# Turning the normalized rows of an adaLN transformer block on VectorE and the DMA queues instead of TensorE

## The chip, the core and the metric

One core of a Trainium2 chip runs the whole program. The time is the device time of one execution in microseconds (us); of the kernel before there are three timed runs, 3591.07, 3591.7 and 3596.67 us, median 3591.7. The engines are named as the profile names them: PE (TensorE matmul), PEld (its weight loads), DVE (VectorE), ACT (ScalarE), POOL (GpSimd) and SP (SyncE, which here issues the DMAs). L201 is line 201 of the kernel before. Where the text speaks of the changed kernel's lines it says so.

## What is computed

The input x has 8 sequences of 1024 tokens of width 512, all float32. Each token passes one transformer block whose two layer norms are modulated by a condition vector:

```python
mod = silu(condition) @ Wada + bada
sh_a, sc_a, gt_a, sh_m, sc_m, gt_m = split(mod, 6, axis=1)
xm = layernorm(x, g1, be1) * (1 + sc_a) + sh_a
x = x + gt_a * attention(xm, Wqkv, Wproj, bproj)      # 16 heads of 32, causal
xm = layernorm(x, g2, be2) * (1 + sc_m) + sh_m
x = x + gt_m * (gelu(xm @ W1 + b1) @ W2 + b2)         # 512 -> 2048 -> 512
```

A layer norm needs a token's 512 numbers in one row (a partition), so that mean and variance run along the row. The matmuls that follow need the numbers transposed: a channel per partition and the tokens along the row. This document is about how the rows are turned.

## The kernel before, in words

**Blocks and sets.** The work is cut into NB = 16 blocks of 512 tokens, two to a sequence. Block n has two sets of normalized rows: a{n} ahead of its attention and m{n} ahead of its MLP, 32 sets in all. A set is 4 tiles of 128 tokens by 512 channels.

**One set.** `normalize` (L547) reads the tiles: mean and variance on DVE (`bn_stats`, `bn_aggr`, L555 and L556), the square root on ACT (L563), reciprocal and offset on DVE (L565, L566), and the normalization as four activations on ACT (L580). ACT holds one table of functions at a time; root, exp and gelu lie in different tables, so a root costs a table load there and the next exp or gelu another. Root and apply are "excursions": jobs that are held back and run one at a time beside an attention unit. `modulated` (L615) then turns the set: for each of 4 chunks of 128 channels, 4 transposes by PE against the identity (L641) into one of the three linear PSUM banks, and one evacuation with gain and shift on DVE (L645) or ACT (L651) into the tile xm. Differences of parts of xm (T1 to T4) follow, which the 7-product (Strassen) form of the matmuls reads.

**Matmuls.** Almost all linear work goes through `matmul` (L194 to L201): four instructions that each fill 32 columns of the array. A product of the 7-product form is 4 such calls, 16 instructions. Float32 matmuls appear twice in the trace, once per pass; the transposes appear once.

**Two streams on PE.** A planner inside the kernel writes out the order of everything by hand. It keeps a modelled clock per engine (`now`), the time at which each datum is written (`written`) and each buffer left (`left`), and prices such as MM = 853 ns for two `matmul` calls and TR = 108 ns for a transpose. The attention stream (`attend`, scores, exp, weights times v, row sums) is written out in its own order; between its units the linear stream (`linear`, the steps of `plan[w]`) is fed in. `step_aside` does linear work as long as attention would wait, or until the linear stream has caught up with its `due`, which grows by each unit's need times a `rate`. The rate is `planned_time(n)`, the summed `costs` of the block's linear steps, over the block's attention need. Steps wait for guards: v of an even block waits until attention has left the block before ("free for v"), the output projection until its block is attended, mt (set m) until v is done.

**Attention's own limits.** Scores and exponents share one PSUM tile (`st`), so each unit waits until DVE has reduced the scores (L1406) or ACT has taken the exponent (L1493). There are three slots for exponents; POOL masks the diagonal ones (L1498) and adds the exponents of a group up (L1594, four additions a unit), and a slot is free only after that. `finish` (L1531) sums over keys by matmuls with ones (L1539), takes the reciprocal on DVE in four parts (L1554) and multiplies. If the linear stream is far away and no bank is in use, `scores_by_heads` (L1357) does a scores unit in the linear banks.

**Weights.** A ring of 9 tiles of 256 KB holds the linear weights. `fetch` (L319) issues a load as soon as the slot's last matmul has been written out; all loads, the x rows and the results are issued by SP in that one order.

Of the kernel before, what the change touches and what calls it, by code (L numbers as in the profile page):

```python
# [9 lines left out]
F32 = mybir.dt.float32  # L10
# [12 lines left out]
def kernel(  # L23
# [173 lines left out]
    def matmul(ps, lhsT, rhs, start, stop, reads=(), bank=None):  # L197

        for j in range(HPG):
            r = slice(j * hd, (j + 1) * hd)  # L200
            nc.tensor.matmul(  # L201
                ps[r, :], lhsT[:, r], rhs, start=start, stop=stop, skip_group_check=True
            )
        n = 1
        for d in rhs.shape[1:]:
            n *= d
        note_pe(2 * COLUMN * n, "columns", reads, [] if bank is None else [("l", bank)])
# [19 lines left out]
    def mlp_steps(n):  # L227
# [7 lines left out]
        + [("mod", 3), ("at", 2), ("v", 1), ("mod", 4), ("columns_m",), ("k", 2), ("gates", "m")],  # L235
    }
    late = []
    for w in range(1, NB):
# [7 lines left out]
        if w == NB - 1:  # L246
            steps = late[:1] + [("load_xr", n)] + rows_a + [("proj", n), ("mt", n)] + late[1:]
            steps += [("v", w)] + rows_m + own + m[3:6]
            late = m[6:]
        else:  # L250

            steps = late + [("v", w), ("load_xr", n)] + rows_a + [("proj", n), ("k", w + 1)]
            if w == 1:
                steps = [("load_xr", n)] + rows_a + [("proj", n)]
            steps += [("mt", n), ("q", w + 1)] + rows_m + own
            at = [("at", w + 2)] if w + 2 < NB else []
            if blocks[w][1] == 0:

                steps += m[3:5]
                late = m[5:6] + at + m[6:]  # L260
            else:
                steps += m[3:6] + at
                late = m[6:]
# [108 lines left out]
    def load_x(n, pool, tag):  # L372
        b, h = blocks[n]
        tiles = []
        for t in range(NTT):
            xt = pool.tile([P, D], F32, tag=tag, name=f"{tag}_{n}_{t}", bufs=NTT)
            nc.sync.dma_start(xt, x[b, h * TB + t * P : h * TB + (t + 1) * P, :])
            tiles.append(xt)
        return tiles

    x_pre = {0: load_x(0, tmp, "hat")}
# [11 lines left out]
    nc.gpsimd.memset(ones, 1.0)  # L393
    minus_ones = const.tile([P, P], BF16, tag="minus_ones", name="minus_ones")
# [23 lines left out]
    def modulation(i):  # L418
        at = take(4)
        part = {kf: halves(j) for kf, j in zip(RAW, at)}  # L420
# [39 lines left out]
    def gates(kind):  # L460

        i, bias = GATES[kind]
        at = take(4)
        part = {kf: halves(j) for kf, j in zip(RAW, at)}
# [44 lines left out]

    pool_jobs = []  # L510
# [23 lines left out]
    def hurry():  # L534

        while jobs and due(jobs[0][1]) <= now["PE"] + 500:
            jobs.pop(0)[0]()
        while excursions and due(excursions[0][1]) <= now["PE"] + 500:
            excursions.pop(0)[0]()
# [4 lines left out]
    def normalize(tiles, key, sources):  # L544
# [6 lines left out]
        got = []  # L551

        def statistics(t):
            st = small.tile([P, nc.vector.BN_STATS_DIM], F32, tag="st", name=f"st_{key}_{t}")
            nc.vector.bn_stats(st, tiles[t])  # L555
            nc.vector.bn_aggr(mv[:, t, :], st)  # L556
            note("DVE", 850, [sources[t]], [("mv", key)])
            if t == NTT - 1:
                excursion(root, [("mv", key)])
                excursion(apply, [("rstd", key)])  # L560
# [8 lines left out]
        def apply():  # L569
            for t, xt in enumerate(tiles):  # L570
                xh = xt
                if key[0] == "m":
                    xh = tmp.tile([P, D], F32, tag="hat", name=f"xh_{key}_{t}", bufs=NTT)
                if key == "a0" and t % 2:
                    nc.vector.tensor_scalar(
                        xh, xt, rstd[:, t : t + 1], offset[:, t : t + 1], ALU.mult, ALU.add
                    )
                    note("DVE", 700, [("rstd", key)], [("hat", key, t)])
                else:
                    nc.scalar.activation(  # L580
                        xh, xt, AF.Identity, bias=offset[:, t : t + 1], scale=rstd[:, t : t + 1]
                    )
                    note_act(800, None, [("rstd", key)], [("hat", key, t)])
                got.append(xh)
            hats[key] = got
# [4 lines left out]
    def normalize_tile(xt, key, t, source):  # L590
# [12 lines left out]
        def apply():  # L603
# [3 lines left out]
            xh = tmp.tile([P, D], F32, tag="hat", name=f"xh_{key}_{t}", bufs=NTT)  # L607
            nc.scalar.activation(xh, xt, AF.Identity, bias=offset, scale=rstd)
            note_act(800, None, [("rstd", key, t)], [("hat", key, t)])
            hats.setdefault(key, []).append(xh)  # L610

        return apply

    def modulated(key, gain, shift, b, guards):
        for t in ("B11", "B21", "B22", "T1", "T2", "T3", "T4"):  # L615
            written[key, t] = NEVER
        yield [("hat", key, 0), *guards], [BANK]
# [15 lines left out]
        at = {t: (key, t) for t in part}  # L633
        for c in range(NC):
            if c:
                yield [("hat", key, 0)], [BANK]
            bank = lin_bank()
            for t in range(NTT):
                if t:
                    yield [("hat", key, t)], []  # L640
                nc.tensor.transpose(banks[bank][:, ts(t, P)], got[t][:, ts(c, P)], ident)  # L641
                note_pe(TR, "whole", [("hat", key, t)], [("l", bank)])
            writes = [at["B11"], at["T1"]] if c < 2 else [at["B21"], at["B22"]]
            if sooner([("l", bank)], writes, 770, 780) == "DVE":
                nc.vector.tensor_scalar(  # L645
                    xm[:, c, :], banks[bank], gain[:, c, b : b + 1], shift[:, c, b : b + 1],
                    ALU.mult, ALU.add,
                )
                note("DVE", 770, [("l", bank)], writes)
            else:  # L650
                nc.scalar.activation(  # L651
                    xm[:, c, :], banks[bank], AF.Identity,
                    bias=shift[:, c, b : b + 1], scale=gain[:, c, b : b + 1],
                )
                note_act(780, None, [("l", bank)], writes)
            live[bank] = False
# [48 lines left out]
    def preparation():  # L705
# [15 lines left out]
        while loaded:  # L721
            if todo:
                load(*todo.pop(0))
            w, i, got, ready = loaded.pop(0)
            for out, a, b, op, name in IN_PLACE:
# [161 lines left out]
    def project_out(n):  # L887
# [48 lines left out]
        if not last:  # L936
            normalize(tiles, f"m{n}", [("xr", n, t) for t in range(NTT)])

    def up(step):
# [16 lines left out]
        if (n, q) == (0, 0):  # L956
            yield ["prepared"], []
# [30 lines left out]
    def down(n, part):  # L988
# [19 lines left out]
        def product(operand):  # L1008
# [3 lines left out]
            for i in range(NQ):  # L1012
                p = next(at)
                for k in range(2):
                    c = 2 * i + k
                    hT = hTs[n, 2 * kh + c // NC][:, c % NC, tokens]
                    for m in range(2):
# [3 lines left out]
                        else:  # L1021
                            yield [], []
                        matmul(
                            banks[bank][:, ts(m, HB)], hT[:, ts(m, P)], halves(p)[:, k, :],
# [45 lines left out]
        if part == 0:  # L1070
            yield [("g", n, 0), ("g", n, 1)], []
# [50 lines left out]
    def perform(step):  # L1122
# [9 lines left out]
        elif kind == "load_xa":  # L1132
            x_pre[step[1]] = load_x(step[1], tmp, "hat")
# [36 lines left out]
        elif kind == "preps":  # L1170
            prepared[0] = [preparation(), 0.0]
            written["prepared"] = NEVER
# [46 lines left out]
    def work():  # L1219

        if linear_wait() == NEVER:
            run_jobs(True)
            run_excursions()
# [6 lines left out]
        run_jobs()  # L1230
        run_pool_jobs()
# [18 lines left out]
    def step_aside(reads, writes):  # L1250
# [14 lines left out]
        run_jobs()  # L1265
        run_pool_jobs()
# [188 lines left out]
    free_p = list(range(3))  # L1455
    outs, totals = {}, {}
# [74 lines left out]
    def finish(n, g):  # L1531
# [3 lines left out]
        step_aside([("acc", n, g)], [BANK])  # L1535
        bank = lin_bank()
        for j in range(HPG):
            r = slice(j * hd, (j + 1) * hd)
            nc.tensor.matmul(banks[bank][r, :], ones[:, :hd], acc[:, j, :], start=True, stop=True)  # L1539
        note_pe(2 * COLUMN * TB, "columns", [("acc", n, g), ("p", slot)], [("l", bank)])  # L1540
        free_p.append(slot)
# [22 lines left out]

        def quotient():
# [16 lines left out]
    def add_weights(n, g, parts, pT, slot):  # L1582

        acc, first = totals[n, g]
# [67 lines left out]
    def close(n, g, parts, pT, slot, last):  # L1652
# [6 lines left out]
        elif parts[0][0] > 0:  # L1659
            free_p.append(slot)  # L1660
        if parts[0][0] == 0:
            totals[n, g] = (pT, slot)
            if (n, g) in shared:
# [3 lines left out]
                free_p.append(slot)  # L1667
# [100 lines left out]
```

## Time and profile before

| | us |
|---|---|
| profiled execution, whole | 3596.93 |
| its span, first to last instruction | 3594.9 |
| median of the three timed runs | 3591.7 |
| PE busy | 3520.8 |
| DVE busy | 2077.3 |
| POOL busy | 2045.1 |
| PEld busy | 1768.4 |
| ACT busy | 1326.4 |

The span is one execution by the hardware profiler. Busy time is the union of an engine's instructions; PE's are pipelined, so that the step from one start to the next, not the duration, tells what an instruction costs PE. The chain of waits follows the work that ended last backwards through whatever released each step. The profile's tables name groups of instructions by line, engine and tile; "idle before" is what the engine waited ahead of them and for whom. The mean granted clock of the execution was 0.993.

### The profile page before, as it was taken

The numbers are of one execution on the slowest core, as the hardware profiler recorded it, in microseconds if no ns is written. First come the engines' busy times: TensorE is split into PE (matmuls) and PEld (weight loads), VectorE is DVE, ScalarE is ACT, GpSimd is POOL, SyncE is SP. The second block draws the span as 40 slices with busy tenths as digits, with TensorE's granted clock in tenths as the row PEclk, the third lists the DMA queues.
The fourth block names the chain that finished last, engine by engine and source line by source line (L and its number), as shares of the span: only waits on it lengthen the run. The fifth ranks groups of instructions, "written<-read, shape, count | busy, mean of one in ns | idle before, by whom it ended". The sixth has DMA issues, their size and how long they took to land.

```text
span 3594.9 us, 120999 instructions
## 1 busy us (share of the span) xinstructions
PE 3520.8 (98%) x54821; PEld 1768.4 (49%) x54821; DVE 2077.3 (58%) x2316; ACT 1326.4 (37%) x1388; POOL 2045.1 (57%) x2187
## 2 busy tenths in 40 slices
PE   8989999999999999999999999999999999999999
PEld 4434445445554455544555445454554545445445
DVE  5766575464755647465464655746557455564663
ACT  2335334253433523335243351424524244232421
POOL 2666745665456754667536665456654566544660
PEclk9989999999999999999999999999999999999999
DMA  6643333434334343433434334343343433335334
GB/s 198 204 133 106 115 98 108 129 100 130 112 113 119 104 131 113 128 98 100 135 108 148 92 95 132 107 142 103 97 128 105 142 101 101 125 93 156 90 112 137
DMA packets 307893, 430.33 MB, mean 120 GB/s; under 512 B 25900, under 2 KB 176236, under 8 KB 307380
## 3 DMA queue, kind: packets, MB, share of 16 engines
q1 hardware_dynamic: 307264, 422.56, 38.6%
q8 instruction: 431, 7.06, 0.8%
q14 instruction: 82, 0.67, 0.1%
q10 hardware_dynamic: 116, 0.03, 0.0%
HBM read 394.12 MB, written 28.38 MB: 118 GB/s over the span
## 4 chain that ended last, share of the span: by engine, by line
PE 88%; DVE 4%; POOL 3%; ACT 3%; issue 1%; DMA 0%; SPq 0%; DVEq 0%; ACTq 0%; POOLq 0%
PE bank L201 61%; PE sc L1389 8%; PE po L1521 7%; PE st L1481 6%; PE st L1469 2%; POOL pT L1594 2%; DVE mx L1406 2%; PE bank L1539 1%; PE bank L641 1%; ACT pT L1493 1%; POOL xr L161 1%; DVE hT L1003 0%; ACT hT L945 0%; DVE xr L158 0%; PE bank L1444 0%
## 5 line engine op out<-in xcount | busy, mean ns | idle before, releaser
L1594 POOL TENSOR_TENSOR pT<-pT,pT 128x384 f32<-128x384 f32 (+2 forms) x1266 | 1196.8, 981 | 393.1 <-PE po L1521 207.2
L1493 ACT ACTIVATE pT<-st 128x2048 f32<-128x2048 f32 x288 | 541.0, 1878 | 849.3 <-PE st L1481 738.7
L201 PE MATMUL bank<-w,hT 128*32 128x256 f32 x14336 | 806.7, 381 | 1.0 <-ACT rec L1545 0.9
L1406 DVE TENSOR_REDUCE mx<-sc 128x4 f32<-128x2048 f32 (+3 forms) x380 | 658.7, 1754 | 144.9 <-PE sc L1389 137.7
L201 PEld LDWEIGHTS bank<-w,hT 128*32 128x32 f32 x14336 | 455.5, 110 | 339.1 <-issue 41.6
L201 PE MATMUL bank<-xm_m,w 128*32 128x256 f32 x8192 | 497.6, 380 | 3.2 <-ACT xm_m L651 3.0
L201 PE MATMUL bank<-t_m,w 128*32 128x256 f32 x6144 | 392.2, 381 | 0.1
L1498 POOL TENSOR_SCALAR_AFFINE_SELECT pT<-pT 128x512 f32<-128x512 f32 x256 | 167.3, 671 | 393.1 <-ACT pT L1493 393.1
L201 PEld LDWEIGHTS bank<-xm_m,w 128*32 128x32 f32 x8192 | 254.4, 110 | 231.9 <-issue 63.5
L1389 PE MATMUL sc<-kT,qT 32*128 32x512 f32 (+3 forms) x3040 | 330.2, 522 | 7.6 <-DVE mx L1406 7.0
L1403 DVE TENSOR_TENSOR sc<-sc,mask 128x1024 f32<-128x1024 f32 (+1 forms) x159 | 161.6, 1016 | 277.2 <-PE sc L1389 243.6
L1521 PE MATMUL po<-pT,v 128*32 128x512 f32 (+3 forms) x3072 | 306.7, 494 | 12.6 <-POOL pT L1498 12.6
L1481 PE MATMUL st<-qT,kT 32*128 32x512 f32 (+3 forms) x3072 | 302.8, 489 | 0.0
L201 PEld LDWEIGHTS bank<-t_m,w 128*32 128x32 f32 x6144 | 187.0, 110 | 197.4 <-issue 78.6
L201 PE MATMUL bank<-xm_a,w 128*32 128x256 f32 x3968 | 242.0, 382 | 0.0
L201 PE MATMUL bank<-w,qT 128*32 128x512 f32 x2048 | 239.4, 598 | 0.0
L1554 DVE RECIPROCAL rec<-rec 128x128 f32<-128x128 f32 x256 | 226.1, 920 | 5.7 <-ACT rec L1545 5.7
L1389 PEld LDWEIGHTS sc<-kT,qT 32*128 32x128 f32 x3040 | 130.4, 184 | 176.0 <-ACT pT L1493 83.2
L201 PE MATMUL bank<-t_a,w 128*32 128x256 f32 x2944 | 189.4, 381 | 0.0
L1493 ACT ACT_TABLE_LOAD x88 | 112.9, 1283 | 203.1 <-PE st L1481 202.6
L193 DVE TENSOR_TENSOR hT<-bank,u_u 128x512 f32<-128x512 f32 x192 | 128.6, 684 | 94.4 <-PE bank L201 93.5
L1425 POOL CAST mcols<-mx 128x16 bf16<-128x16 f32 x63 | 16.5, 262 | 290.7 <-DVE mx L1420 160.5
(207 smaller groups left out, 3640.8 us busy)
## 6 DMA issues: line engine op xcount, KB each, us to landing
w<-in_L_cond_W_dram SPq DMA_DIRECT2D x384, 256.0 KB
w<-kept_up_S SPq DMA_DIRECT2D x256, 256.0 KB
w<-kept_down_S SPq DMA_DIRECT2D x256, 256.0 KB
w<-kept_qkv_S SPq DMA_DIRECT2D x180, 256.0 KB
w<-in_L_cond_Wqkv_dram SPq DMA_DIRECT2D x147, 256.0 KB
hat<-in_x_dram SPq DMA_DIRECT2D x64, 256.0 KB
w<-in_L_cond_Wproj_dram SPq DMA_DIRECT2D x64, 256.0 KB
xr<-in_x_dram SPq DMA_DIRECT2D x64, 256.0 KB
```

The lines of the kernel that those rows point to most:

```text
L193: nc.vector.tensor_tensor(out, src, other, op)
L201: nc.tensor.matmul(ps[r, :], lhsT[:, r], rhs, start=start, stop=stop, skip_group_check=True)
L1389: nc.tensor.matmul(sc[:, j, c0 : c0 + w], qTs[n][r, gg, ts(qt, P)], keys_of(n, kh)[r, gg, :w], start=True, stop=True, skip_group_check=True,)
L1403: nc.vector.tensor_tensor(place, place, shape_of.to_broadcast(place.shape), ALU.add)
L1406: nc.vector.tensor_reduce(maxima[n, gg][:, kh, qt, :], sc[:, :, c0 : c0 + w], axis=AX.X, op=ALU.max)
L1469: nc.tensor.matmul(st[:, j, c0 : c0 + w], minus_ones[r, :], row[r, TB - w :], start=(c0 == 0), stop=False, skip_group_check=True,)
L1481: nc.tensor.matmul(st[:, j, c0 : c0 + w], kT[r, gg, ts(k % NTT, P)], qT[r, gg, TB - w :], start=False, stop=True, skip_group_check=True,)
L1493: nc.scalar.activation(pT[:, :, :used], st[:, :, :used], AF.Exp, scale=scale)
L1498: nc.gpsimd.affine_select(diagonal, diagonal, pattern=[[0, HPG], [1, P]], compare_op=ALU.is_ge, fill=0.0, base=0, channel_multiplier=-1,)
L1521: nc.tensor.matmul(po[r, TB - w :], v[:, k % NTT, g * P + j * hd : g * P + (j + 1) * hd], pT[:, j, c0 : c0 + w], start=(k == 0), stop=last ...
L1554: nc.vector.reciprocal(some, some)
L1594: nc.gpsimd.tensor_tensor(into, into, pT[:, j, c0 : c0 + w], ALU.add)
```

## The change

Sets a0, a1, m0, m14 and m15 are still turned by PE. The other 27 (a2 to a15, m1 to m13) are turned thus: each of the 4 row tiles is transposed on DVE in squares of 32 by 32 into the tile xm, which serves as staging; 16 DMAs of 32 partitions by 2 KB, issued by SP, gather the squares from xm back into the set's row tile, where channels then lie along the partitions; and the evacuation with gain and shift reads that tile in SBUF, not PSUM. So that the squares fall right, x rows of the turned a sets are loaded with 32 partitions per tile of 128 tokens, and the tokens of the turned m sets stay permuted, which `down` undoes by the order in which it takes its stationary columns. The four row tiles become one tile, hat, with one buffer.

After the opening, the root is no activation: POOL computes (variance + eps) to the power -0.5 and the offset in four small instructions. The four applications become jobs of their own that go to DVE or ACT, whichever the planner thinks sooner.

In block 0's last head group the three later exponent tiles are not added on POOL; PE sums them with the first by more matmuls with ones, and the quotient is taken on DVE.

Some steps move. k of block 2 goes from the plan of block 0 to that of block 1, ahead of proj 0; mt goes ahead of k in later blocks; u of block 0 waits only for the up weights ("prepared up").

```diff
-            steps = late + [("v", w), ("load_xr", n)] + rows_a + [("proj", n), ("k", w + 1)]
+            steps = late + [("v", w), ("load_xr", n)] + rows_a + [("proj", n), ("mt", n), ("k", w + 1)]
             if w == 1:
-                steps = [("load_xr", n)] + rows_a + [("proj", n)]
-            steps += [("mt", n), ("q", w + 1)] + rows_m + own
+                steps = [("load_xr", n)] + rows_a + [("k", w + 1), ("proj", n), ("mt", n)]
+            steps += [("q", w + 1)] + rows_m + own
...
+    by_pe = ("a0", "a1", "m0", f"m{NB - 2}", f"m{NB - 1}")
+    def hat_tile(key):
+        return tmp.tile([P, NTT, D], F32, tag="hat", name=f"hat_{key}", bufs=1)
...
+        def power():
+            nc.gpsimd.tensor_scalar(rstd, mv[:, :, 1], EPS, None, ALU.add)
+            nc.gpsimd.tensor_tensor(rstd, rstd, minus_half, ALU.pow)
+            nc.gpsimd.tensor_scalar(offset, mv[:, :, 0], -1.0, None, ALU.mult)
+            nc.gpsimd.tensor_tensor(offset, offset, rstd, ALU.mult)
+            note("POOL", 1500, [("mv", key)], [("rstd", key)])
...
+    def turn(key, rows, xm):
+        small_blocks = xm.rearrange("p c n -> p (c n)")
+        by_tile = small_blocks.rearrange("p (m h t i) -> p h m t i", m=NTT, h=NC, t=NTT)
+        def turn_tile(t):
+            into = by_tile[:, :, :, t, :]
+            nc.vector.transpose(into, rows[:, t, :].rearrange("p (h m i) -> p h m i", m=NTT, i=Q))
+            note("DVE", 620, [("hat", key, t)], done)
+        for t in range(NTT):
+            add_job(lambda t=t: turn_tile(t), [("hat", key, t)], key[0] == "m")
+        yield [("blocks", key)], []
+        for m in range(NTT):
+            for a in range(NTT):
+                nc.sync.dma_start(rows[ts(m, Q), a, :], small_blocks[ts(a, Q), ts(m, D)])
+        written["turned", key] = now["PE"] + GATHERING
+        yield [("turned", key)], []
+    GATHERING = 9000
...
         for c in range(NC):
+            if turned:
+                source, out = ("turned", key), xm[:, c, :].rearrange("p (a x) -> p a x", x=P)
+                values = got[:, :, ts(c, P)]
+            else:
...
...
+        terms = [(0, TB, acc, slot)] + [(c0, w, pT, slot) for parts, pT, slot in more for _, c0, w, _ in parts]
+        for i, (c0, w, term, held) in enumerate(terms):
+            for j in range(HPG):
+                nc.tensor.matmul(
+                    banks[bank][r, TB - w :], ones[:, :hd], term[:, j, c0 : c0 + w],
```

The line `costs = {"at": 16 * TR, "mt": 16 * TR, ...}`, from which the linear stream's rate comes, is not changed.

## Prediction

> **What bounds the kernel.** The page first: the busy line and PE's slices.
>
> ```profile
> PE 3520.8 (98%) x54821; PEld 1768.4 (49%) x54821; DVE 2077.3 (58%) x2316; ACT 1326.4 (37%) x1388; POOL 2045.1 (57%) x2187
> ...
> PE   8989999999999999999999999999999999999999
> ...
> PEclk9989999999999999999999999999999999999999
> ...
> PE 88%; DVE 4%; POOL 3%; ACT 3%; issue 1%; DMA 0%; SPq 0%; DVEq 0%; ACTq 0%; POOLq 0%
> ```
>
> PE is busy 98% and carries 88% of the chain that ended last; DVE has 1518 us to spare and ACT 2269. Work taken off PE shortens the run unless something new makes PE wait, and PE's 74 us of idle time are the most that any other edit could win. So I read second what a transpose costs PE, in the timeline of PE: set a4, turned without a break, and the two halves of set m1.
>
> ```profile
> 844.53 2.18 PE L641 MATMUL bank<-ident,hat 128*128 128x128 f32 x16
> 846.73 0.85 PE L201 MATMUL bank<-w,hT 128*32 128x256 f32 x11
> ...
> 504.98 1.09 PE L641 MATMUL bank<-ident,xh_m 128*128 128x128 f32 x8
> 506.50 0.64 PE L201 MATMUL bank<-xm_m,w 128*32 128x256 f32 x8 [0.43 <-ACT xm_m L651]
> ```
>
> The step from the first transpose to the next matmul is the price: 846.73 - 844.53 = 2.2 us a set. The second half of m1 took 1.52 for 8, of which 0.43 is waiting for the evacuation. Third, the windows view of the slow stretch near the start (columns: window, length, busy and count of PE, PEld, DVE, ACT, POOL, granted clock, DMA share, GB/s).
>
> ```profile
> 177.00:207.00 30.00, 20.00 (x108) 8.05 (x106) 28.29 (x36) 2.46 (x2) 15.64 (x15) 0.60 0.82 285
> 400.00:430.00 30.00, 29.33 (x492) 15.77 (x488) 19.76 (x18) 5.58 (x5) 26.97 (x28) 0.97 0.36 105
> ```
>
> Between 177 and 207 PE is idle a third of the time and runs at a granted clock of 0.60; DVE is full: the linear stream is waiting for block 0 to be attended, and scores alone go on at DVE's pace. At 400 to 430 POOL is nearly full (27.0 of 30) and PE is kept busy by linear work.
>
> **The change, term by term** (us of span; plus is slower).
>
> 1. *Transposes off PE.* 27 sets of 16 leave. The 12 sets a4 to a15 cost 2.2 each (26). a2 and a3, cut up by waits for evacuations, cost 3.4 and 4.6 in their timelines (8). The m sets alternate between two halves of 1.02 and 1.52 (2.54; m1 and six more) and 12 + 4 at 1.73 and 0.59 (2.32; six): 18 + 14 = 32. Sum 66; some of the waiting in it will return as waiting elsewhere, so **-63**, bounds -47 (432 bare transposes at 0.109, the usual step) and -70 (with 0.11 for the switch into each run, the step before it being 0.31 and not 0.20).
>
> 2. *The hole at 177 to 207.* At full clock and without gaps its instructions would take about 10 of the 30 us. The changed order puts 28 calls of k(2) and the projection between the scores, 2.6 to 4.5 us of PE work after each unit against DVE's 3.0 to 3.6 (2.29 to reduce, 0.66 to 1.21 for the mask). The exponent sums on PE spare POOL 12 additions and cost PE three more terms, 4 x (0.17 + 0.11 + 0.06) = 1.4. Together **-15**, bounds -20 and 0 (the hole stays).
>
> 3. *The hole moves.* k(2) was what kept the end of block 1 supplied. In the changed order of PE's instructions, the last five exponent units around the end of block 1 and three scores units have no linear instruction between them, 14.5 us of PE work by the steps above. There each unit is paced by POOL: four additions of 512 columns at
>
> ```profile
> L1594 POOL TENSOR_TENSOR pT<-pT,pT 128x512 f32<-128x512 f32 x504 | 648.6, 1320 | 223.8 <-ACT pT L1493 183.3 <-PE po L1521 38.0
> ```
>
> 1.32 make 5.3 a unit. From the group's second unit to its sum POOL has 3 x 5.3 + 6 (diagonal) + 7 (the cut ones) = 29; PE's work there is 15 to 19: **+14**, bounds +6 and +24 (with a lowered clock after it).
>
> 4. *Smaller holes.* `costs` still charges the linear stream 16 TR for each at and mt, so the rate is 3.5 us a block too high and linear work runs ahead until a guard stops it. The order shows three such stretches more (two of three or four units ahead of the first products of m3 and m7, one of five at block 15's start): each unit takes its PE work, 1.15, and 1.88 for the exponent (L1493), or 0.96 and 2.3 for the reduction, with nothing beside it: **+8**, bounds +3 and +16.
>
> 5. *The end.* Now 80 linear instructions (8.9 us) lie between the last sum with ones and the last projection, and 88 more between that sum and the last unit ahead of it. In the changed order all of them come earlier and none stands after the last unit: PE waits for its exponent (1.9), its masks (1.2) and POOL's and DVE's additions (3.5): **+6**, bounds 0 and +10.
>
> 6. *The gather's wait.* Added per set: 4 transposes on DVE, then 16 issues on SP, the landing, and the evacuation. No row shows a 32 by 32 transpose; the nearest, 128x512 from SBUF to SBUF, are 0.54 (L575) and 1.70 (L1591, beside POOL); I take 0.65. No row shows a DMA within SBUF either. An issue takes 0.34 (median duration of L337) to 0.68:
>
> ```profile
> 650.56 2.04 SPq L1145 DMA_DIRECT2D xr<-in_x_dram  x3
> ```
>
> so 16 take 5.4 to 10.9, nearest 0.47 (the median step between xr's issues) = 7.5. A landing took 6.4 in the chain's DMA step at 8.22 us, with all queues full; bounds 0 and 6.4, I take 2.5, since the DMA engines are 38% busy and the pieces are a quarter of that size. Gather: 10, bounds 5.4 and 17. The issues stand behind weight loads that themselves wait for PE:
>
> ```profile
> SPq L337 <- PE bank L201: 1616.8, 643, 19.7
> ```
>
> so a gather cannot start before PE gets to that place. a sets have 11 us or more of PE work between evacuation and use: no wait. For the 13 m sets the order leaves between 7 and 16 us from the gather's first issue to the first product, which needs 10 + 0.8 (one evacuation, 0.78): about 0.8 each, **+10**, bounds 0 and 13 x 7 = 90 at worst. Behind the gather in SP's queue wait weight loads; the ring's 9 tiles cover 9 x 1.78 = 16 us of bare linear work, so 7.5 us of issues are hidden unless DVE's last transpose is itself late.
>
> 7. *Cover.* DVE gains 108 x 0.65 + 41 applications at 0.54 + 14 evacuations at 0.81 = 103 and loses 29 reciprocals and offsets (some 14): about 61% busy. ACT loses 29 roots, 41 applications at 0.80 and 77 of 177 table loads:
>
> ```profile
> L563 ACT ACT_TABLE_LOAD x29 | 37.2, 1283 | 0.4
> ```
>
> -99 in loads and -42 besides. POOL gains 116 small operations; 128x16 rows take 0.24 to 0.31, the power is in no row (0.24 to 1.3, bound by a 512-wide one): 30 to 65, against 9 for the additions. None is on the path in the steady part: **0**, bounds -8 (exponents come sooner) and +5.
>
> The Trainium skill speaks both ways. "DMA: Bandwidth & Descriptors", section Bandwidth, says that transfers under 64 KB are dominated by descriptors and asks for 1 MiB a DMA, and its anatomy of one DMA gives about 2.0 us fixed for each; here a set's 1 MiB goes in 16 pieces of 64 KB, and if each ended before the next began the gather would take about 34 us by that page, an estimate, and term 6 some +300. The trace speaks for overlap (issues follow each other after 0.47 with earlier loads under way), which the term uses. "Vector Engine (DVE) Microarchitecture Reference", section 3.8, says that the 32x32 transpose keeps up one element per cycle and lane; no run here shows it yet.
>
> **Sum.** -63 - 15 + 14 + 8 + 6 + 10 + 0 = -40. The profiled execution took 3596.93 with a span of 3594.9; it is like the highest of the three timed runs (3596.67) and 5.2 over their median. Span after: about 3555; from the median: 3591.7 - 40 = **3552**.
>
> **Rivals.**
>
> *A. The gather is the new wait.* Each us by which DVE's transposes, the issues and the landing are later than my 0.8 at the 13 m sets costs 13. From 40 / 13 = 3.1 more on, that is 3.9 a set or a gather of 13, within its bounds, the gain is gone. At 6 a set: 3552 + 13 x 5.2 = 3620. For it: 16 issues behind a queue that waits for PE, no row for such a DMA. Against: the order of PE has 7 to 16 us of other work in hand at each of them. Slower than before; 0.13.
>
> *B. The holes cost double.* Terms 3, 4, 5 at their upper bounds, and half of term 2 lost because DVE, now fuller, still paces the scores: -40 + 10 + 8 + 4 + 8 = -10, 3582. For it: the linear stream is charged too much and so runs dry. 0.18.
>
> *C. The waits cancel.* No gather wait, holes at their lower bounds: -40 - 10 - 8 - 5 - 6 = -69, 3523. For it: 99 us of table loads leave ACT, which ends exponent waits. 0.14.
>
> *D.* That the transposes do not leave PE is excluded: 432 of 512 are gone from its order.
>
> **Numbers.** Forecast 0.55 (3552, its own range 3532 to 3572). The range that leaves out the worse half of A and the better third of C is 3515 to 3592. What a measurement here can tell from no change is about 0.2%, 7 us: faster means under 3584.5. Faster: 0.55 + 0.14 + two thirds of B's 0.18 = 0.80; same: the rest of B and a little of A, 0.08; slower 0.12.
>
> **What would show it.** L641's group falls from 512 to 80 transposes and PE's busy time by some 55; the window 177 to 207 has a granted clock near 1.0; PE idles around the end of block 1 behind POOL's additions, with a dip of the clock there; PE's waits for xm_m are ten or so of about 1 us, not 4; the issues at the gather step by about 0.47. Wrong would be: gather issues at 0.7 or more, PE waiting for xm_m at every m set, or weight loads late behind the gather.

## The result, and the profile after

The changed kernel took 3639.95 us (median of four, 3631.70 to 3645.93), the kernel before 3591.48 (median of four, 3591.07 to 3596.67): 1.0128 times as long, 95% interval 1.0115 to 1.0141. The forecast was 3552, the range up to 3592: wrong in sign. The profiled execution of the changed kernel took 3631.7 with a span of 3630.0, so the sums below explain +35.1 of span; the medians are 48 apart.

From the page of the changed kernel: busy line and chain, as shown of before.

```profile
PE 3489.7 (96%) x54413; PEld 1733.5 (48%) x54413; DVE 2199.7 (61%) x2463; ACT 1195.3 (33%) x1246; POOL 2078.1 (57%) x2240
...
PE 78%; SPq 6%; DVE 5%; POOL 5%; ACT 2%; DMA 2%; issue 2%; ACTq 0%; DVEq 0%; POOLq 0%
```

PE's busy time fell by 31, its idle time rose from 74.1 to 140.3: +66 - 31 = +35. A second thing is the clock: the stretches in which the trace has it at half add up to 99.1 us against 51.9 before. They come in pieces of 3.41 us behind gaps in PE's work, and make the same work up to (99.1 - 51.9) / 2 = 24 longer. Without them PE's work would be up to 55 shorter, as forecast. In the chain SPq is new: 6% of the span went by way of SP's queue, and DMA has 2%.

The windows view (window, length, busy and count of PE, PEld, DVE, ACT, POOL, granted clock, DMA share, GB/s), two rows of the changed kernel and then the second window in the kernel before:

```profile
177.00:207.00 30.00, 30.00 (x357) 11.46 (x358) 24.71 (x26) 1.76 (x3) 18.69 (x20) 0.94 0.58 186
387.00:417.00 30.00, 18.62 (x184) 7.13 (x176) 18.33 (x31) 9.53 (x6) 28.26 (x26) 0.89 0.10 33
```

```profile
387.00:417.00 30.00, 27.06 (x392) 13.72 (x388) 22.97 (x19) 10.35 (x9) 29.92 (x22) 0.94 0.24 66
```

The hole near the start is closed (PE 30.0 of 30 where it was 20.0 at clock 0.60). At the end of block 1 there is one instead: PE busy 18.6 of 30 where it was 27.1, POOL 28.3.

Groups and waits of the changed kernel: the new operations, and the waits of ACT and DVE for the gathers of a sets (total, times, longest).

```profile
L662 DVE STREAM_TRANSPOSE xm_a<-hat_a 128x512 f32<-128x512 f32 x56 | 35.2, 676 | 0.0
...
L604 POOL TENSOR_TENSOR rstd_m<-rstd_m,minus_half 128x4 f32<-128x4 f32 x15 | 15.7, 1047 | 1.2
```

```profile
ACT xm_a L730 <- DMA hat_a<-xm_a: 106.1, 13, 16.4
...
DVE xm_a L724 <- DMA hat_a<-xm_a: 55.8, 11, 9.0
```

A transpose in squares is 0.68 us (0.65 was taken), the power 1.05 us for 4 numbers a partition. The last two lines are the ones to stop at: ACT stood idle 106 us in 13 waits for a gather, up to 16.4 at a time, and DVE 56. An idle engine is no loss by itself. What stands behind the waiting instruction is, so next the timeline of one a set: SP, then ACT, then PE.

```profile
1069.96 11.87 SPq L671 DMA_DIRECT2D hat_a<-xm_a  x16
...
1083.42 2.23 ACT L730 ACTIVATE xm_a<-hat_a,shifta,gaina 128x512 f32<-128x512 f32 x3 [13.11 <-DMA hat_a<-xm_a]
1085.55 0.56 ACT L188 COPY p_v<-bank 128x512 f32<-128x512 f32 x1
...
1079.86 1.91 PE L202 MATMUL bank<-w,t_a 128*32 128x256 f32 x32
1086.17 5.01 PE L202 MATMUL bank<-w,xm_a 128*32 128x256 f32 x64 [4.40 <-ACT p_v L188]
```

The 16 issues take 11.9 us and the data are there 13.5 after the first. ACT has been waiting at the first evacuation for 13.1 us. Behind that and two more evacuations in its queue stands the copy of p_v, a product of v that PE finished by 1081.8. PE needs that bank: 4.4 us idle. At other a sets it is the second thing in that list, the weight load behind the issues:

```profile
1521.23 11.23 SPq L671 DMA_DIRECT2D hat_a<-xm_a  x16
...
1533.18 0.91 SPq L340 DMA_DIRECT2D w<-in_L_cond_Wproj_dram  x2
...
1536.29 4.54 PE L202 MATMUL bank<-w,qT 128*32 128x512 f32 x24 [6.94 <-DMA w<-in_L_cond_Wproj_dram]
```

Here PE has p_v, runs through v, and waits 6.9 us for a weight whose load could not be issued before 1533. And an m set:

```profile
939.14 11.28 SPq L671 DMA_DIRECT2D hat_m<-xm_m  x16
...
942.68 1.14 PE L1479 MATMUL sc<-kT,qT 32*128 32x512 f32 x8
...
946.83 0.69 PE L1447 MATMUL bank<-kT,qT 32*128 32x512 f32 x1 [2.15 <-DVE mx L1466]
...
952.78 1.96 PE L202 MATMUL bank<-xm_m,w 128*32 128x256 f32 x32 [0.56 <-DVE xm_m L724]
```

The last linear work ends at 942.7, the next needs xm_m, which is there at 952.7. In those ten microseconds attention is alone and goes at the pace of DVE's reductions. The wait that names xm_m is 0.56 us; what the gather costs stands under other names, as waits for mx (DVE's maxima of the scores).

### The profile page after: what moved, and what is told of

Same layout as the page of the kernel before. It is cut to its first block, busy times and chain, and to the rows that moved or that the text cites. A ratio compares the mean times of both kernels' runs of the same rounds, so it can differ in the third digit from the quotient of the medians.

```text
span 3630.0 us, 120959 instructions
## 1 busy us (share of the span) xinstructions
PE 3489.7 (96%) x54413; PEld 1733.5 (48%) x54413; DVE 2199.7 (61%) x2463; ACT 1195.3 (33%) x1246; POOL 2078.1 (57%) x2240
## 4 chain that ended last, share of the span: by engine, by line
PE 78%; SPq 6%; DVE 5%; POOL 5%; ACT 2%; DMA 2%; issue 2%; ACTq 0%; DVEq 0%; POOLq 0%
PE bank L202 55%; PE sc L1479 7%; PE st L1572 6%; PE po L1612 6%; SPq L671 6%; POOL pT L1702 3%; PE st L1560 2%; PE bank L1633 2%; DVE mx L1496 1%; ACT pT L1584 1%; DMA hat_m<-xm_m 1%; POOL hT L161 1%; DMA hat_a<-xm_a 1%; ACT xm_a L730 0%; DVE xr L158 0%
## 5 line engine op out<-in xcount | busy, mean ns | idle before, releaser
L1702 POOL TENSOR_TENSOR pT<-pT,pT 128x256 f32<-128x256 f32 (+3 forms) x1254 | 1225.3, 1012 | 304.7 <-PE po L1612 183.2
L202 PE MATMUL bank<-w,hT 128*32 128x256 f32 x14336 | 817.7, 380 | 0.0
L202 PEld LDWEIGHTS bank<-w,hT 128*32 128x32 f32 x14336 | 446.9, 110 | 381.5 <-issue 98.1
L202 PE MATMUL bank<-t_m,w 128*32 128x256 f32 x6144 | 381.6, 381 | 2.4 <-DVE qT L193 2.0
L1676 POOL TENSOR_TENSOR qT<-top,rec 128x512 f32<-128x512 f32 x61 | 80.2, 1316 | 218.9 <-DVE rec L1651 196.3
L202 PEld LDWEIGHTS bank<-xm_a,w 128*32 128x32 f32 x3968 | 124.6, 111 | 107.2 <-issue 29.5
```

The source lines that it names most:

```text
L202: nc.tensor.matmul(ps[r, :], columns, rhs, start=start, stop=stop, skip_group_check=True)
L1702: nc.gpsimd.tensor_tensor(into, into, pT[:, j, c0 : c0 + w], ALU.add)
```

## Experiments

Sixteen kernels, each beside the kernel before on its chip. Median in us, ratio to before with its 95% interval:

| run | what | us | ratio |
|---|---|---|---|
| e1_all_pe | all sets on PE, the other edits kept | 3578.2 | 0.9962 (0.9948 to 0.9976) |
| e2_m_only | only m sets gathered | 3585.5 | 0.9978 (0.9969 to 0.9987) |
| e3_a_only | only a sets gathered | 3626.6 | 1.0096 (1.0081 to 1.0111) |
| e4_act_queue | change, gather issued by ACT | 3704.4 | 1.0313 (1.0298 to 1.0328) |
| e5_pieces | change, issues by fours | 3731.1 | 1.0386 (1.0371 to 1.0402) |
| e8_late16 | change, plan takes 16 us | 3624.7 | 1.0090 (1.0075 to 1.0106) |
| e6_dram16 | the same by way of DRAM | 3610.5 | 1.0051 (1.0036 to 1.0066) |
| e9_late16_costs | e8, lower rate | 3652.2 | 1.0169 (1.0152 to 1.0186) |
| e10_a_late16 | e3, plan takes 16 us | 3584.2 | 0.9976 (0.9967 to 0.9986) |
| e11_a_dram16 | e10 by way of DRAM | 3559.4 | 0.9913 (0.9898 to 0.9928) |
| e16_a4_dram16 | e11, a2 and a3 on PE | 3553.4 | 0.9891 (0.9876 to 0.9905) |
| e17_m_late16 | e2, plan takes 16 us | 3575.6 | 0.9957 (0.9940 to 0.9973) |
| e15_m_no_gather | e2 without the gather: its rows stay unturned | 3541.9 | 0.9859 (0.9844 to 0.9873) |
| e12_pe_steps | e1, steps as before | 3597.4 | 1.0015 (1.0006 to 1.0024) |
| e13_pe_root | e1, root on ACT | 3595.0 | 1.0009 (1.0000 to 1.0019) |
| e14_pe_pooladd | e1, sums on POOL | 3590.9 | 0.9993 (0.9984 to 1.0002) |

### Which sets cost

The first theory, read from the stretch at 1521: weight loads stand behind the gather in SP's queue and PE runs dry.

```diff
-    by_pe = ("a0", "a1", "m0", f"m{NB - 2}", f"m{NB - 1}")
+    by_pe = [f"{kind}{n}" for kind in "am" for n in range(NB)]                     # e1_all_pe
+    by_pe = [f"a{n}" for n in range(NB)] + ["m0", f"m{NB - 2}", f"m{NB - 1}"]      # e2_m_only
+    by_pe = [f"m{n}" for n in range(NB)] + ["a0", "a1"]                            # e3_a_only
```

e1_all_pe: 

> All 32 sets are turned by PE again; the power on POOL, the sums on PE and the moved steps stay. Theory (the gathers stand ahead of weight loads in SP's one queue, at the a sets above all, and PE runs dry and then at half clock): the change's 98 us beyond its own good terms were gaps at the a sets 39, clock 25, waits of the m sets 20 and a rest; they go, the transposes come back with 63: 3600 to 3620. Rival 1 (the moved steps and the holes of the linear stream cost it, not the gather): the transposes are added to the loss, 3670 or more.

e2_m_only: 

> Only the 13 m sets are turned by VectorE and gathered; all a sets by PE. Theory (weight loads late behind the gathers of the a sets): gaps and half clock of the a sets go, 64 to 75, and 34 of transposes come back: about 3604. Rival 2 (what costs is the wait for the gather itself at the m sets): nothing is won and 34 come back: 3674.

e3_a_only: 

> Only the 14 sets a2 to a15 are turned by VectorE and gathered; all m sets by PE. Theory: the m sets' waits of some 20 go, 32 of transposes come back: about 3652, no better than the change. Rival 2 (the wait for the gather at the m sets): 98 go and 32 come back: about 3575.

With all sets on PE it is 3578, 62 under the change and 14 under before: the loss is the turning's, and the other edits are a gain, more than the theory had. Turning only the m sets adds 7 to 3578, only the a sets 48. So the a sets are the worse, but the m sets win nothing either. The second rival had 3674 for the m-only run, 88 too much, and 3575 for the a-only run, 52 too little; the theory missed by 18 and 25. So the m sets' wait is not the whole of it, and the theory is off too. PE's waits in the a-only run show what it is about:

```profile
PE bank L202 <- ACT p_v L188: 39.2, 10, 5.6
...
PE bank L202 <- DMA w<-in_L_cond_Wproj_dram: 5.7, 1, 5.7
...
PE bank L202 <- DMA w<-kept_qkv_S: 1.6, 1, 1.6
```

Ten waits of about 4 us are for p_v, two are for a weight of these products. That speaks against the first theory.

### Another queue

```diff
-                nc.sync.dma_start(rows[ts(m, Q), a, :], small_blocks[ts(a, Q), ts(m, D)])
+                nc.scalar.dma_start(rows[ts(m, Q), a, :], small_blocks[ts(a, Q), ts(m, D)])
```

> The same 16 DMAs a set, issued by ACT and not by SP: no weight load stands behind them, and they stand behind no weight load. Theory: gaps of the a sets and their clock go: 3560 to 3580, and L671's issues are gone from the waits of PE. Rival 3 (the gather's bytes hold the DMA engines, whichever queue issues them): 3630 to 3640 as before. Against both stands the price of the test: ACT is held for 16 issues a set, some 10 us in which no exponent is taken; if attention has no cover for it, each of 27 sets loses up to 5 us, and the time is 3640 to 3700 with PE waiting for ACT.

3704, beyond the price given there. The timeline of ACT at one a set:

```profile
637.07 13.77 ACTq L671 DMA_DIRECT2D hat_a<-xm_a  x16
654.34 2.93 ACT L730 ACTIVATE xm_a<-hat_a,shifta,gaina 128x512 f32<-128x512 f32 x4 [19.18 <-DMA out_dram<-xr]
657.18 0.56 ACT L188 COPY p_v<-bank 128x512 f32<-128x512 f32 x1
```

No weight load stands behind a gather here, and PE still waits for p_v, 6.4 us at this set. The gather is no shorter on another queue: 13.8 us of issues, and the evacuation could start 17.3 after the first. (The view names a store as what ended that wait, but the evacuation reads hat_a, which the gather writes.) The Trainium skill, "DMA: Bandwidth & Descriptors", section Queues, rings and completion order, says that SP's and ACT's queues are rows on the same DMA engines, with none of their own; the lengths, 10 to 16 us for 16 issues by ACT and 10.4 to 12.2 by SP, do not speak against it.

### The plan's landing time

A new theory: ACT and DVE take their work in order, and the plan puts the evacuations where the gather should have landed after `GATHERING` = 9 us; the trace has 11.8 to 14.2. Whatever is behind them is late by the difference and more.

```diff
-    GATHERING = 9000
+    GATHERING = 16000                                                    # e8_late16
...
             for a in range(NTT):
                 nc.sync.dma_start(rows[ts(m, Q), a, :], small_blocks[ts(a, Q), ts(m, D)])
+            if m < NTT - 1:                                              # e5_pieces, GATHERING = 1500
+                written["piece", key, m] = now["PE"] + 2500
+                yield [("piece", key, m)], []
```

e8_late16: 

> One number: the planner takes a gather to need 16 us from its issue to its landing, not 9 (12 to 14.3 in the trace of the changed kernel). Instructions and DMAs are the same; evacuations of turned sets come later in the order of ACT and DVE. New theory (ACT and DVE stand still in their queues at an evacuation whose gather has not landed, and behind it stands the evacuation of a product that PE needs): PE's gaps of 3 to 7 us at the a sets go, with the half clock after them; 3640 becomes 3550 to 3580. First theory (weight loads late behind the gather in SP's queue): the issues are where they were, 3630 to 3640.

e5_pieces: 

> The 16 issues of a gather go out by fours, with at least 2.5 us of the planned PE time between, so that weight loads come between them in SP's queue; the planner's landing is 1.5 us after the last piece, that is 9 after the first as before. First theory (weight loads late behind 11 us of issues): the a sets' gaps go, 3570 to 3590. New theory (evacuations stand too early in ACT's and DVE's order): the landing comes no earlier and the plan still takes it for 9, so the gaps stay, 3630 to 3660, named as waits for ACT's p_v.

In pieces the gather lands 13 to 24 us after its first issue while the plan still has about 9, and the time is 3731: the more the landing is behind the plan, the longer the run, though weight loads can now pass between the pieces. With 16 us ACT's waits for gathers of a sets fall from 106 us to 21 and PE waits for p_v no more, but only 15 of the hoped 60 to 90 come back. Both theories had the wrong size; something else was left, and the two kinds of sets had to be taken apart.

### The a sets alone

```diff
+    GATHERING = 16000, by_pe as in e3_a_only                             # e10_a_late16
...
-        for m in range(NTT):
-            for a in range(NTT):
-                nc.sync.dma_start(rows[ts(m, Q), a, :], small_blocks[ts(a, Q), ts(m, D)])
+        scratch = kept.tile([P, NTT * D], F32, tag="turn", name=f"turn_{key}", bufs=2)
+        nc.sync.dma_start(scratch, small_blocks)                         # e11_a_dram16
+        for m in range(NTT):
+            nc.sync.dma_start(
+                rows[ts(m, Q), :, :], scratch[:, ts(m, D)].rearrange("(a i) x -> i a x", i=Q))
```

e10_a_late16: 

> Only a2 to a15 turned by VectorE, and the planner's 16 us for a gather; against the run with only a sets at 9 us (3626.6). Theory (evacuations too early in ACT's queue, with ACT idle 12 to 20 us ahead of them there): the wait for p_v goes at all 14 sets; beside the run with all sets on PE (3578.2), 34 of transposes are saved: 3544 if nothing else is late, up to 3565 with some weight loads late. First theory (weight loads behind 11 us of issues): 3615 to 3630. Rival 3 (a 16 us turn is too long for the a sets too, so that attention is left alone as at the m sets): 3590 to 3610.

e11_a_dram16: 

> As the run with a sets only and 16 us, but the gather goes by way of DRAM in 5 issues (about 7 us in SP's queue, landing after 13 to 14) and not 16 (11 us, landing after 13). If weight loads behind the issues are late in that run, this one is 5 to 20 us faster; if not, the two are within 5.

One number moves the a-only run from 3626.6 to 3584.2: 42 us. The planner works out the whole order anew from it, so that PE's instructions are interleaved otherwise too; but the waits for p_v and v, 45 us of PE in e3_a_only, are gone. ACT at the set of the timeline above, in e10_a_late16: p_v goes first, the evacuations after it, and none waits for the gather.

```profile
1073.90 0.59 ACT L188 COPY p_v<-bank 128x512 f32<-128x512 f32 x1 [15.41 <-PE bank L202]
...
1077.84 2.22 ACT L730 ACTIVATE xm_a<-hat_a,shifta,gaina 128x512 f32<-128x512 f32 x3
```

With that gone the first theory's mechanism comes out from under it. PE's waits for weights in e10_a_late16, then in e11_a_dram16:

```profile
PE bank L202 <- DMA w<-kept_qkv_S: 13.2, 10, 2.1
PE bank L202 <- DMA w<-in_L_cond_Wproj_dram: 9.1, 13, 2.1
```

```profile
PE bank L202 <- DMA w<-kept_qkv_S: 3.5, 4, 1.6
PE bank L202 <- DMA w<-in_L_cond_Wproj_dram: 3.5, 6, 1.7
```

By way of DRAM the data land no sooner (12 to 15 us), and twice the bytes are moved, but SP is through earlier and with 5 issues:

```profile
1061.92 0.38 SPq L670 DMA_DIRECT2D turn_a<-xm_a  x1
1066.98 1.74 SPq L672 DMA_DIRECT2D hat_a<-turn_a  x4
1068.82 0.38 SPq L338 DMA_DIRECT2D w<-kept_qkv_S  x1
```

6.9 us from the first issue to the next weight load, not 12.4 as in e10_a_late16, and that is worth 25 us of time. So both mechanisms were there, one behind the other. The Trainium skill, "DMA: Bandwidth & Descriptors", section Bandwidth, asks for few large DMAs; here they win, by what their issues hold up and not by a shorter transfer. The fixed 2 us of the same page's anatomy of one DMA, which it fits on DMAs issued by GpSimd, never added up 16 times: all 16 had landed after 12 to 14 us.

### The m sets

```diff
+        for m in range(0):                                    # e15_m_no_gather: no DMA, landing = now
...
+    GATHERING = 16000, by_pe as in e2_m_only                  # e17_m_late16
```

e15_m_no_gather: 

> As the run with m sets only (3585.5), but the squares are not gathered: the 16 DMAs of each m set are left out and the evacuation reads the normalized rows unturned (so the computation leaves out the turning; all other instructions stay). Theory (PE has no linear work left while the 13 us gather of an m set runs): the waits at the m sets go, and beside the run with all sets on PE (3578.2) the 32 of transposes are won: 3540 to 3555. Rival 4 (VectorE's own 2.7 us a set and its port hold the reductions up, not the gather): 3575 to 3585.

e17_m_late16: 

> As the run with m sets only, with the planner's 16 us. At the m sets the next product itself needs the set, so a later evacuation in ACT's queue helps little: 3578 to 3588, against 3585.5. If ACT's and DVE's queues were the cause here as at the a sets: 3545 to 3560.

Without the gather 3541.9: 43.6 less than with it, 3.4 for each of 13 m sets, and 36 less than with all sets on PE, which is what the 13 sets of transposes cost there (32 was the estimate). PE's idle time goes from 91.6 to 64.4 and the half clock from 58.5 to 18.1 us. VectorE's transposes are still in that run, so they are not the price. Weight loads behind the gather are not it either: in e2_m_only PE waits for no weight after the first 120 us (6.1 us of waits before). The plan's landing time gives only 10: for the rest it is the time of the gather that counts here, not the order. An m set lies between the output projection and the product that needs it, with k and q of a later block as the only linear work beside it, and the gather with its wait adds 13 us to that path.

### What else was planned around it

e6_dram16: 

> Against the run with 16 us: the gather goes by way of DRAM, one DMA of 1 MiB out and four of 256 KB back, 5 issues instead of 16, the second four waiting in SP's queue for the first to land. If the issues at 0.6 to 0.7 set the 12 us of the gather, five of them take 3 and two landings of 3 to 6 remain: 9 to 15 us, time within 10 of that run; if bytes set it (twice as many), 20 us or more and weight loads behind the wait late: 3640 or more.

e9_late16_costs (`costs` charges 0 for at and mt): 

> Against the run with 16 us: the planner's costs charge nothing for at and mt, so the linear stream's rate is 3.5 us a block lower, as it would be with no transposes on PE. If the smaller holes of the prediction's fourth term come from the overcharge, 3 to 16 us less than that run; if they come from evacuations or the order, within 5 of it; if the lower rate leaves linear work over at the ends of blocks, slower by 5 to 20.

By way of DRAM with all 27 sets wins 14 over e8_late16, not the 25 of the a sets. The lower rate loses 27, and PE's waits for DVE's maxima of the scores grow from 53 to 72 us; that linear work kept back by the rate was missed there fits this, but is not shown.

These waits also tell where part of the loss in e8_late16 is. Its largest row of them, then the same row of e10_a_late16:

```profile
PE st L1560 <- DVE mx L1496: 30.6, 23, 6.1
```

```profile
PE st L1560 <- DVE mx L1496: 8.0, 4, 6.1
```

With the other rows it is 53 us with both kinds of sets turned, 12 with the a sets alone, 21 with the m sets alone (e17_m_late16) and 9 with none. PE is left with attention alone more often when both kinds are turned.

### The other edits, one taken back at a time

```diff
+    plan, mt and k(2) as before the change                     # e12_pe_steps
+    excursion(root, [("mv", key)]) instead of power()          # e13_pe_root
+    first_end, unadded = None, []                              # e14_pe_pooladd
```

e12_pe_steps: 

> All sets on PE, and the steps in the order of the kernel before: k of block 2 in block 0's plan, mt behind k. Power on POOL and the sums on PE stay. If the moved steps won what the run with all sets on PE won (14 against the kernel before, of which the prediction's second term gave 15 to the hole at 177 to 207), this one is at 3588 to 3592; if the power and the placing of the applications won it, it stays at 3576 to 3581.

e13_pe_root: 

> All sets on PE, and the root back on ACT as an excursion (29 roots, with a table load each and a load after it), reciprocal and offset on DVE. The prediction's seventh term (some 140 us off ACT, none on the path): within 4 of 3578. If the table loads had been on attention's path: 3585 to 3595.

e14_pe_pooladd: 

> All sets on PE, but block 0's last group is summed on POOL again, as before. If the prediction's second term is right that POOL's 12 additions hold up the start of block 1: 3586 to 3592, with a hole and a lowered clock at 177 to 210; if the moved steps alone closed that hole: 3576 to 3581.

Taken back alone, each loses 13 to 19: steps 19, power 17, sums 13. All three together win only 14 against the kernel before, so these are not parts of a sum: leaving any one out loses about the whole gain. The window from 177 to 207 in e1_all_pe, e12_pe_steps and e14_pe_pooladd:

```profile
177.00:207.00 30.00, 30.00 (x364) 11.09 (x360) 22.48 (x27) 5.91 (x6) 22.74 (x25) 1.00 0.82 286
```

```profile
177.00:207.00 30.00, 16.96 (x152) 5.12 (x144) 14.66 (x15) 0.00 (x0) 6.84 (x6) 0.77 0.67 221
```

```profile
177.00:207.00 30.00, 20.57 (x144) 8.37 (x148) 22.80 (x31) 4.34 (x3) 12.68 (x13) 0.77 0.56 205
```

Either of steps and sums missing opens the hole again: with both in place, the 9 to 13 us of idle PE in this window are gone. With the root back on ACT the window stays full (30.0 of 30, clock 1.00); its 17 us are spread over the run, 13.6 more of idle time and 12.8 more at half clock. That run has 177 table loads on ACT, not 119, but reciprocal and offset are back on DVE too, so it does not show the loads alone as the cause.

### A faster version

> Only a4 to a15 turned by VectorE and gathered by way of DRAM, 16 us; a2 and a3 on PE. With a sets from a2 on it was 3559.4, with 7.5, 5 and 1.7 us of idle PE at 385 to 419, against 2.3, 3.6 and 1.7 with all sets on PE. If that hole comes from turning a2 and a3, 12 to 18 are won and some 6 of transposes lost: 3545 to 3553; if it comes from the rate of the linear stream or the moved step, 3560 to 3568.

```diff
+    by_pe = [f"m{n}" for n in range(NB)] + ["a0", "a1", "a2", "a3"]      # beside e11_a_dram16's edits
```

3553.4, 38 us under before and the best of those that compute the whole block; 12 of the 32 sets are turned off PE. Its busy line:

```profile
PE 3494.8 (98%) x54653; PEld 1742.2 (49%) x54653; DVE 2166.7 (61%) x2377; ACT 1208.9 (34%) x1254; POOL 2088.2 (59%) x2248
```

PE is idle 55.7 and at half clock for 17.0 us; in the change it was 140.3 and 99.1. Against all sets on PE it wins 24.8, and 12 sets at 2.2 are 26: nearly every transpose that left is now time won.

## Why the prediction was wrong

The turning, terms 1 and 6, was put at -53 and measured +62; all else, terms 2 to 5 and 7, was put at +13 and measured -14 in the run with all sets on PE. So the larger error, 115 us, is in the turning.

**Term 1, transposes off PE (-63): right.** Twelve a sets gave 24.8 of the 26 estimated, thirteen m sets 36 where 32 was estimated.

**Term 6, the gather's wait (+10): this is the step that failed, at three places.** The run with all sets on PE and the change differ by 62, and some 66 of transposes are in it: 24.8 + 36, and 2.2 or a little more for each of a2 and a3. So the gathers cost about 128, where the term had 10. What each place costs is from the runs with one kind of set turned:

- "a sets have 11 us or more of PE work between evacuation and use: no wait." The use was looked at, not the queue. The evacuation stands in ACT's order, waits there for the landing, and holds up the copy of a product. This is 42 us of a-set time, shown by one number of the plan, with the waits for p_v gone. The prediction asked what is queued behind the waiting instruction for SP; for ACT and DVE it did not.
- "The ring's 9 tiles cover 9 x 1.78 = 16 us of bare linear work, so 7.5 us of issues are hidden unless DVE's last transpose is itself late." An issue takes 0.70 on average (11.3 for 16), not 0.47, and the ring did not cover it: in the stretch at 1521 PE was out of work at 1529.4, and the load of the weight it needed was issued at 1533.2. 25 us, shown by 5 issues for 16 with a landing no earlier. The prediction's own sign for this case, issues at 0.7 or more and weight loads late behind the gather, came true.
- "about 0.8 each" for the 13 m sets. It is 3.4 each, 44 us. The gather takes 12 to 14 us and not 10; and that PE finds attention units to run in the meantime is less than it seems, since alone they go at DVE's pace. It is rival A's mechanism and near its price (from 3.9 a set the gain is gone), though only the smaller part of the loss; the larger lay at the sets that the rival did not count. The sign that was to tell came true and told nothing: PE's waits for xm_m are nine, 10 us in all, and the rest stands as waits for mx and as half clock.

42 + 25 + 44 = 111 of 128. Of the rest, some 10 went with turning a2 and a3 (e16_a4_dram16 is 6 faster and has two sets' transposes back, 4.5). What is left is not accounted for. In the changed kernel itself the first two could not be won back at these prices: plan and DRAM together took it from 3640 to 3610 only, 29 and not 67. For with the plan at 16 us the m sets add 40 to e10_a_late16, but take 3 off e1_all_pe. The trace of e8_late16 has PE waiting for DVE's maxima there, as told above; why linear work runs out sooner with both kinds turned is open.

**The clock.** The prediction had no term for it outside the holes, and took PE's 74 us of idle time for the most that other edits could win. In the changed kernel's trace, after the first 30 us, every gap of PE of 2.4 us and more was followed by 3.4 to 10.2 us at half clock, and of those of about 2 us some, which made 66 us more of idle time into up to 90 of loss.

**Term 2 (-15): right in place, its size in line.** PE is busy all through 177 to 207, and either of its two halves taken back costs 13 or 19; but these runs hold more than this window.

**Term 3, the hole moves (+14): right in place, a little high, half right in cause.** PE is idle 11.4 us of 387 to 417 and the clock is 0.89; before it was idle 2.9 at 0.94, so the move cost 8.4 and some 2 of clock. With k(2) moved and all sets on PE, 6.6 are idle (23.36 busy); the other part came from a2 and a3 (13.0 idle in e11_a_dram16, 6.6 in e16_a4_dram16).

**Term 4, smaller holes from the overcharged rate (+8): refuted.** With the charge taken away from e8_late16 the run was 27 slower.

**Term 5, the end (+6): right in size, not in cause.** From the timeline of PE at the end:

```profile
3492.02 0.40 PE L1560 MATMUL st<-mrow,minus_ones 32*128 32x384 bf16 x8 [1.01 <-ACT pT L1584]
...
3499.83 1.93 PE L1612 MATMUL po<-pT,v 128*32 128x384 f32 x16 [5.50 <-POOL pT L1589]
3503.42 2.38 PE L1633 MATMUL bank<-pT,ones 128*32 128x512 f32 x8 [1.65 <-POOL pT L1702]
```

1.0 + 5.5 + 1.65 = 8.2 of idle time, behind the exponent, the masks and the additions, as named. But PE waited there before too, 2.3 for the masks and 0.9 for ACT's copy of the sums, so that 5 are new, and 10.2 us at half clock follow, worth up to 5. The same steps with all sets on PE, or with one kind of set turned, leave the waits as before (1.9 to 2.0 and 0.9): the cost came only with both kinds turned.

**Term 7, cover (0): wrong in the other direction.** The root back on ACT, with its table loads and with reciprocal and offset on DVE, costs 17: this work was not all beside the path.

**Rivals B and C** do not describe it. Without term 6 the sum would have been -50; the best version has -38, with 12 of the 27 sets turned. That this is near the forecast's -40 is chance.

## What to carry to other kernels

Where work moves from an engine to a transfer, the transfer's latency has to be placed in the order of every engine that handles its result: ask what stands behind the instruction that waits for it, on that engine, before asking when the result is used. In a kernel with an order written by hand, a planned latency that is too short can cost by itself (42 us here, with the same gathers), and a DMA's issues count as time on the queue that the next loads share. Take a move apart by where it lands: here the turning won 2 us a set at a4 to a15, once plan and issues were mended, and won 3 us in all, at best, at the m sets, where the next product waits for it.

## What the runs showed of the hardware

- An issue of a 32-partition, 64 KB DMA within SBUF takes 0.70 us on average in a row of 16 (10.4 to 12.2 us a row), and the row lands 1.4 to 3.3 us after its last issue ends; the issues of 256 KB weight loads from DRAM have medians of 0.32 to 0.40. The same row issued by ACT took 10 to 16 us.
- One MB from SBUF to DRAM and back in 5 DMAs is there after 12 to 15 us (e11_a_dram16), as late as 16 DMAs within SBUF, 12 to 14 (e10_a_late16).
- The 32 by 32 transpose of 128x512 on VectorE takes 0.68 us, as much as a subtraction of that size (0.69). The Trainium skill, "Vector Engine (DVE) Microarchitecture Reference", section 3.8, has it at one element per cycle and lane; the two equal rows agree with that.
- POOL takes 1.05 us to raise 128x4 numbers to a power, and 0.20 to 0.24 to add or multiply them.
- After gaps of PE of 2.4 us and more, and after some of about 2, the clock halves for 3.41 us or a multiple of it in the changed kernel's trace: 99 us there, 17 in the best version's.
